# Attention scores in runs of nine over a ring of seven PSUM banks, with eight summed key blocks

## The chip, the core and the metric

The kernel runs on one core of a Trainium2 chip. The metric is the device time of one execution in microseconds, as the median of several runs. A core has a matrix engine (PE, TensorE; its weight loads are shown as PEld), a vector engine (DVE), a scalar engine (ACT), a general engine (POOL, GpSimd) and a sync engine (SP), and 16 DMA engines that the queues of SP and POOL share. Matrix products land in PSUM, which has eight banks of 512 fp32 numbers per partition; the rest lives in SBUF.

## The reference

Two layers are applied to an image tensor `x` of shape (2, 256, 64, 64). The change is in the first, which is plain attention over the 4096 pixels of each of the two images, with 8 heads of 32 channels:

```python
x = x + _L0_conv_ref(_gn(x), L0_conv_qkv_w, L0_conv_qkv_b, 8)

qkv = jnp.einsum('bchw,oc->bohw', x, qkv_w) + qkv_b[None, :, None, None]
qkv = qkv.reshape(b, 3, num_heads, head_dim, n)
q, k, v = (qkv[:, 0], qkv[:, 1], qkv[:, 2])
attn_logits = jnp.einsum('bhci,bhcj->bhij', q, k) * scale
attn_weights = jax.nn.softmax(attn_logits, axis=-1)
out = jnp.einsum('bhij,bhcj->bhci', attn_weights, v)
```

The second layer (group attention and a convolution over the result) is not changed.

## The kernel before

`attention0` handles one image. Its work is cut into 16 groups `g`: a head and one half of the 4096 queries, as four tiles of 512 queries. A group runs over 32 key blocks `j` of 128 keys. A **unit** is one key block against one query tile: a matmul of 128 keys by 512 queries, which fills one PSUM bank with scores. There are 16 x 32 x 4 = 2048 units for each image. A unit passes through these steps:

- PE writes the scores into a PSUM bank (`scores`, L505).
- ACT takes the exponential out of PSUM into SBUF (L511). The exponentials live in a ring of 28 places (`RING`), 17 of them in the tile `es` and 11 in the tile that also holds the values (shown as `v` in the profile). `at_places` splits an activation where the ring changes tile or wraps.
- PE multiplies them with the values and adds up in the bank `av` (`quarters`, L521), four query tiles side by side in four column groups of 32.
- For the softmax's denominator the exponentials of all key blocks have to be added. DVE adds most blocks into two tiles `e` (`add_rows`, L558). A few blocks of each group, listed in `SUMMED`, are added by POOL's accumulating DMAs into four tiles `acc` instead (`add_in_memory`, L566 for the first, which copies, and L568 for those that accumulate). At the start of the next group DVE adds `acc` to `e` (L748), and a matmul with ones sums over the partitions into a spare bank.

**Before**, `scores` issues seven units at a time into three PSUM tiles: `sa` of three banks, `sb` of two and `sc` of two, with one activation for each tile:

```python
for tag, size in (("sa", 3), ("sb", 2), ("sc", 2)):
    ...
    sc = psum["sc"].tile([P, size, T], F32, tag=tag, name=f"{tag}_{b}_{first}")
```

The eighth bank is `av`. When a spare bank is wanted (row sums of the group before, statistics of the next layer), `sa` is filled with two units and its third bank is lent.

The order on PE, ACT and DVE is written out by hand (`tc.manual_schedule`, from L771). Each turn of the loop issues one run of scores and then value products (`steps`, `work_of`) in half blocks: until the share that belongs to the scores issued so far is reached, and at least as many as `must` says, so that places of the ring that are about to be overwritten have been read. Value products work on units of earlier runs, never of the run just issued. DVE's additions stand in the order in which `work_of` asks for them. SP and POOL are ordered by the framework. SP fetches the next head's keys and values in every second group (`fetch_head`, asked for at `j == 4` of even groups) and the queries of the group after the next (`fetch_queries`).

A place of the ring is written again 28 places later. Before ACT may do so, PE's value product, DVE's addition and, in a summed block, the DMA that reads it must be done. An accumulating DMA waits for the one before it into the same tile of `acc`.

Of the kernel before, what the change touches and what calls it, by code (L numbers as in the profile page):

```python
# [9 lines left out]
F32 = mybir.dt.float32  # L10
I32 = mybir.dt.int32
F32R = mybir.dt.float32r
AF = mybir.ActivationFunctionType
# [4 lines left out]
P = 128  # L18
B, C, H, W = 2, 256, 64, 64
N = H * W  # L20
T = 512
# [4 lines left out]
NH0 = C // HD0  # L26
# [14 lines left out]
def direct_layers(ctx: ExitStack, tc: tile.TileContext, a: dict, out: bass.AP, bad: bass.AP):  # L41
# [3 lines left out]
    nc = tc.nc  # L45
# [11 lines left out]
    psum = {}  # L57
# [307 lines left out]
    SC0 = 1.0 / math.sqrt(HD0)  # L365
# [8 lines left out]
    NJ = N // P  # L374
# [76 lines left out]

    RING, RING_A = 28, 17

    SUMMED = (3, 7, 11, 15, 18, 22, 26)

    def summed(g):

        return SUMMED if g else SUMMED[1:]

# [4 lines left out]
    def attention0(b, xts, held):  # L464
# [10 lines left out]
        n_units = NH0 * 2 * NJ * 4  # L475
# [4 lines left out]
        places = []  # L480
        n_places = 0

        def at_places(first, n):

            while n > 0:
                at = first % RING
                m = min(n, (RING_A if at < RING_A else RING) - at)
                yield m, es[:, at : at + m, :] if at < RING_A else held["es"][:, at - RING_A : at - RING_A + m, :]
                first, n = first + m, n - m

        def scores(spare):

            nonlocal n_places
            bank = None
            for tag, size in (("sa", 3), ("sb", 2), ("sc", 2)):
                first = len(places)
                n = min(size - (spare and size == 3), n_units - first)
                if n <= 0:
                    break
                sc = psum["sc"].tile([P, size, T], F32, tag=tag, name=f"{tag}_{b}_{first}")  # L500
                if spare and size == 3:
                    bank = sc[:, size - 1, :]
                for i in range(n):
                    g, (j, u) = (first + i) // (4 * NJ), divmod((first + i) % (4 * NJ), 4)
                    nc.tensor.matmul(  # L505
                        sc[:, i, :], held["k", g // 2][:, j * P : (j + 1) * P], held["q", g, u // 2][:, u % 2, :],
                        start=True, stop=True,
                    )
                i = 0
                for m, dst in at_places(n_places, n):  # L510
                    nc.scalar.activation(dst, sc[:, i : i + m, :], AF.Exp, scale=SC0)  # L511
                    i += m
                places.extend(range(n_places, n_places + n))
                n_places += size
            return bank

        def quarters(dst, lhs, rhs, start, stop, part=None):

# [17 lines left out]
        def add_rows(g, j):  # L536
            if j == 0:
                sums[g] = psum["sc"].tile([P, T], F32, tag="av", name=f"av_{b}_{g}")
                added[g] = [w4([P, 2, T], f"e_{b}_{g}_{w}") for w in range(2)]
                return  # L540
            for w in range(2):
                dst = added[g][w]
                if j in summed(g):
                    if w == 0:
                        add_in_memory(g, j)
                    continue
                if j == 1:
                    first = two_units(g, 0, w), two_units(g, 1, w)
                    if len(first[0]) == len(first[1]) == 1:
                        nc.vector.tensor_add(dst, first[0][0][1], first[1][0][1])  # L550
                    else:
                        for s in range(2):
                            nc.vector.tensor_add(dst[:, s, :], unit(g, 0, 2 * w + s), unit(g, 1, 2 * w + s))
                    continue
                for s, src in two_units(g, j, w):
                    if g == last and j in SUMMED_LAST:
                        continue
                    nc.vector.tensor_add(dst[:, s, :], dst[:, s, :], src)  # L558
# [11 lines left out]
        def work_of(g, j):  # L570


            if (g, j) < (last, NJ - 3):
                add_rows(g, j)
            for part in (None,) if j in (0, NJ - 1) else range(2):
                if part == 1:
                    yield
                quarters(
                    sums[g], held["v"][:, (g // 2) % 2, j, :], lambda u: unit(g, j, u), j == 0, j == NJ - 1, part
                )  # L580

        def sum_rows(g, rows):
            if g == last:
                for part in range(2):
                    for j in SUMMED_LAST:
                        quarters(rows, ones, lambda u: unit(g, j, u), j == SUMMED_LAST[0], False, part)
                    quarters(rows, ones, lambda u: acc[u], False, False, part)
                    quarters(rows, ones, lambda u: added[g][u // 2][:, u % 2, :], False, True, part)
                return
            quarters(rows, ones, lambda u: added[g][u // 2][:, u % 2, :], True, True)  # L590
# [140 lines left out]
        def steps():  # L731

            for done in range(NH0 * 2 * NJ):
                g, j = divmod(done, NJ)
                if (g, j) == (last, NJ - 3):
                    assert len(places) == n_units
                    held["rows"] = psum["sc"].tile([P, 3, T], F32, tag="sa", name=f"rows_{b}")[:, 2, :]
                    for i in (NJ - 3, NJ - 2, NJ - 1):
                        add_rows(g, i)
                    sum_rows(g, held["rows"])  # L740
                for _ in work_of(g, j):
                    yield done
                if g and j == 0:

                    for w in range(2):
                        dst = added[g - 1][w]
                        for s in range(2) if w == 0 else (slice(0, 2),):
                            nc.vector.tensor_add(dst[:, s, :], dst[:, s, :], acc[s] if w == 0 else pair)  # L748
                    waiting.clear()
                if g and j == 1:  # L750
                    wanted.append(late[0].send)
                if g and j in (9, 17):
                    next(late[0])
                for what in also.get((g, j), ()):
                    what()
                if j == 4 and g % 2 == 0 and g // 2 + 1 < NH0:
                    fetch_head(b, g // 2 + 1, held)
                if j == NJ - 1:
                    waiting.append(g)
                    avs = w4([P, 2, T], f"avs_{b}_{g}")  # L760
                    if g < last:
                        nc.scalar.copy(avs[:, 0, :], sums[g])
                    copied[g] = avs
                    late[:] = [finish(g)]
                    next(late[0])
                    if g + 2 < NH0 * 2:
                        fetch_queries(b, g + 2, held)
                yield done + 1

        E = mybir.EngineType  # L770
        with tc.manual_schedule(engines={E.PE, E.Activation, E.DVE}):  # L771

            per_group = 2 * NJ - 2
            work, begun, taken = steps(), 0, 0
            scores(False)
            final = False
            while not final:
                have = len(places)  # L780
                use = wanted.pop(0) if wanted else None
                bank = scores(use is not None)
                final = have == n_units
                ready = have // 4
                share = have * per_group // (4 * NJ) - 2

                must = sum(place < n_places + 7 - RING for place in places[: 4 * ready : 4])
                if must % NJ == 1:
                    must += 1
                assert must <= ready  # L790
                here = 0
                while begun < ready and (taken < share or begun < must or final or use is not None):
                    if use is not None and here == 2:
                        use(bank)
                        use = None
                        continue
                    here += 1
                    group = begun // NJ
                    begun = next(work)
                    taken += 1  # L800
                    if begun // NJ > group and begun >= must and not final and use is None:
                        break
                if use is not None:
                    use(bank)
            assert next(work, None) is None
            return *finish_last(last), st
# [585 lines left out]
    for b in range(B):  # L1392
        xts = x_first if b == 0 else ahead["xts"]
        w0 = w0_first if b == 0 else ahead["w0"]
        with tc.tile_pool(name=f"ps0_{b}", bufs=8, space=PSUM) as psum["ps"]:
# [7 lines left out]
            held = project0(b, xn, w0)  # L1403
# [571 lines left out]
```

## Time and profile before

| | us |
|---|---|
| median of 3 runs | 3118.44 (3115.47 to 3122.96) |
| span of the profiled execution | 3116.4 |
| attention of the first image, first to last instruction | 118.4 to 1161.1 |
| attention of the second image | 1666.3 to 2709.4 |

| engine | busy us, whole span | share |
|---|---|---|
| PE | 3031.2 | 97% |
| DVE | 2467.0 | 79% |
| ACT | 2313.6 | 74% |
| POOL | 836.7 | 27% |

| group of instructions | count | mean ns |
|---|---|---|
| L505 scores, PE, `sa` / `sb` / `sc` | 1736 / 1180 / 1180 | 430 / 396 / 396 |
| L521 value products, PE, 256 queries | 15360 | 383 |
| L511 exponentials, ACT, two banks | 1180 in `sb` and `sc` | 1020 to 1037 |
| L511 exponentials, ACT, three banks | 556 | 1457 |
| L558 additions, DVE, 1024 wide | 1332 | 1216 |

A value product appears twice in the trace[...]. The durations of neighbouring instructions on one engine overlap, so that the distance from start to start, and not the duration, is what one of them costs in a full queue. DMA engines are busy for 80% of both attention stages.

### The profile page before, as it was taken

What the parts mean: (1) busy time and instruction counts of PE and PEld (TensorE: products, weight loads), DVE (VectorE), ACT (ScalarE), POOL (GpSimd) and SP (SyncE); (2) the same over time, 40 slices, a digit from 0 to 9 for tenths busy, and PEclk for the clock granted to TensorE, in tenths of its full rate; (3) what the DMA queues carried; (4) which work ended last, traced back from release to release, by engine and by line L of the source; (5) the groups of instructions that cost most, each with busy time, mean ns of one, the idle gap of its engine ahead of it and who ended that gap; (6) DMA issues with size and microseconds to landing.
All of it is one profiled execution on the core that took longest, in us unless ns stands there. A gap on an engine that the chain in (4) does not pass through costs nothing. (4 is left out here: it accounts for less than half of the span.)

```text
span 3116.4 us, 62659 instructions
## 1 busy us (share of the span) xinstructions
PE 3031.2 (97%) x25129; PEld 1830.6 (59%) x25129; DVE 2467.0 (79%) x3126; ACT 2313.6 (74%) x2436; POOL 836.7 (27%) x923
## 2 busy tenths in 40 slices
PE   6999999999999999999989999999999999999998
PEld 4555555555555556677755555555555555476765
DVE  4599989999899999856556998989989999834543
ACT  2699999999999984622237999999999999734333
POOL 2022222222222231055301222222222222305440
PEclk9999999999999999999999999999999999999999
DMA  7969679797897761230159687796888975700000
GB/s 241 270 132 185 143 150 172 154 178 150 164 181 154 145 133 33 75 134 29 41 193 268 128 176 151 156 176 138 177 162 164 181 153 123 170 4 4 21 14 22
DMA packets 243787, 424.41 MB, mean 136 GB/s; under 512 B 99112, under 2 KB 109916, under 8 KB 241308
## 3 DMA queue, kind: packets, MB, share of 16 engines
q0 software_dynamic: 94992, 238.36, 39.8%
q1 hardware_dynamic: 147580, 181.68, 21.6%
q8 instruction: 199, 3.26, 0.4%
q14 instruction: 104, 0.85, 0.1%
q10 hardware_dynamic: 912, 0.27, 0.0%
HBM read 119.03 MB, written 68.39 MB: 60 GB/s over the span
## 5 line engine op out<-in xcount | busy, mean ns | idle before, releaser
L558 DVE TENSOR_TENSOR e<-e,es 128x1024 f32<-128x1024 f32 (+1 forms) x956 | 1038.6, 1142 | 79.6 <-ACT es L511 77.9
L521 PE MATMUL av<-es,v 128*32 128x256 f32 (+1 forms) x9644 | 746.7, 390 | 0.0
L558 DVE TENSOR_TENSOR e<-e,v 128x1024 f32<-128x1024 f32 (+1 forms) x640 | 675.2, 1107 | 47.7 <-ACT v L511 46.6
L511 ACT ACTIVATE es<-sa 128x1536 f32<-128x1536 f32 (+1 forms) x444 | 635.7, 1432 | 93.1 <-PE sa L505 54.9
L505 PE MATMUL sa<-q,k 128*128 128x512 f32 x1736 | 561.4, 430 | 9.2 <-ACT avs L598 3.5
L521 PE MATMUL av<-v 128*32 128x256 f32 (+1 forms) x6228 | 506.5, 389 | 0.0
L521 PEld LDWEIGHTS av<-es,v 128*32 128x32 f32 x9644 | 316.1, 109 | 299.4 <-issue 160.6
L505 PEld LDWEIGHTS sa<-q,k 128*128 128x128 f32 x1736 | 280.0, 188 | 291.8 <-issue 135.4
L505 PE MATMUL sc<-q,k 128*128 128x512 f32 x1180 | 371.4, 396 | 1.7 <-ACT es L511 0.7
L505 PE MATMUL sb<-q,k 128*128 128x512 f32 x1180 | 371.0, 395 | 1.1 <-ACT es L511 1.1
L521 PEld LDWEIGHTS av<-v 128*32 128x32 f32 x6228 | 216.5, 109 | 178.6 <-issue 81.2
L511 ACT ACTIVATE es<-sc 128x1024 f32<-128x1024 f32 x296 | 306.9, 1037 | 0.0
L511 ACT ACTIVATE v<-sc 128x1024 f32<-128x1024 f32 x294 | 304.9, 1037 | 0.1
L511 ACT ACTIVATE es<-sb 128x1024 f32<-128x1024 f32 x296 | 302.0, 1020 | 3.8 <-DMA acc<-es 3.8
L511 ACT ACTIVATE v<-sb 128x1024 f32<-128x1024 f32 x294 | 300.0, 1020 | 0.0
L505 PEld LDWEIGHTS sb<-q,k 128*128 128x128 f32 x1180 | 221.2, 188 | 55.4 <-ACT es L511 2.9
L505 PEld LDWEIGHTS sc<-q,k 128*128 128x128 f32 x1180 | 210.5, 188 | 71.8 <-ACT es L511 12.1
L511 ACT ACTIVATE v<-sa 128x1536 f32<-128x1536 f32 (+1 forms) x146 | 209.2, 1433 | 35.6 <-PE sa L505 17.0
L948 PE MATMUL mm<-v,wf 128*128 128x256 f32 x1024 | 227.6, 380 | 1.5 <-DVE z L957 1.5
L568 POOL DMA_DIRECT2D es<-es x116 | 98.9, 853 | 475.6 <-ACT es L511 424.3
L948 PEld LDWEIGHTS mm<-v,wf 128*128 128x128 f32 x1024 | 193.3, 190 | 36.8 <-issue 9.9
L938 POOL TENSOR_TENSOR v<-col 128x512 f32<-128x512 f32 x128 | 165.1, 1316 | 179.2 <-ACT rk_sr L1089 39.2
(262 smaller groups left out, 3179.0 us busy)
## 6 DMA issues: line engine op xcount, KB each, us to landing
acc<-es POOLq DMA_DIRECT2D x128, 512.0 KB, 6.2
acc<-v POOLq DMA_DIRECT2D x84, 512.0 KB, 6.4
es<-es POOLq DMA_DIRECT2D x136, 256.0 KB, 4.5
v<-es POOLq DMA_DIRECT2D x132, 256.0 KB, 5.1
k<-wk_halves SPq DMA_DIRECT2D x64, 512.0 KB
q<-wq_halves SPq DMA_DIRECT2D x256, 128.0 KB
v<-v POOLq DMA_DIRECT2D x90, 256.0 KB, 5.4
es<-v POOLq DMA_DIRECT2D x86, 256.0 KB, 3.9
```

The lines of the kernel that those rows point to most:

```text
L505: nc.tensor.matmul(sc[:, i, :], held["k", g // 2][:, j * P : (j + 1) * P], held["q", g, u // 2][:, u % 2, :], start=True, stop=True,)
L511: nc.scalar.activation(dst, sc[:, i : i + m, :], AF.Exp, scale=SC0)
L521: nc.tensor.matmul(dst[HD0 * u : HD0 * u + HD0, n], lhs, rhs(u)[:, n], start=start, stop=stop)
L558: nc.vector.tensor_add(dst[:, s, :], dst[:, s, :], src)
L568: nc.gpsimd.dma_start(out=dst, in_=src, accum_op=ALU.add)
L938: (nc.gpsimd.tensor_add if plus else nc.gpsimd.tensor_sub)(dst, rows(one), rows(two))
L948: nc.tensor.matmul(mm[:, m, r, :], wf[:, k, 4 * r + q, m * P : (m + 1) * P], v[r // 2][:, r % 2, k, :], start=k == 0, stop=k == KC - 1,)
```

## The change

`sa`, `sb` and `sc` become one PSUM tile `ring` of seven banks, used in turn. A turn of the loop now issues nine units, in activations of 1, 1, 3, 2 and 2 banks (`PHASE`). Where such a part crosses the end of the ring of banks, or the end of a tile of exponentials, it is cut in two (`runs_of`). A spare bank is the next one of the ring and takes up one place. The loop keeps the value products at least seven units behind the scores (`behind`), and may carry on with them to the end of a group (`ending`). The list of summed blocks goes from seven of 32 key blocks to eight; in the first group of an image the first of the list is left out, as before.

```diff
-    SUMMED = (3, 7, 11, 15, 18, 22, 26)
+    SUMMED = (3, 6, 10, 13, 17, 20, 24, 27)
...
-        def scores(spare):
+        BANKS = 7
+
+        PHASE = (1, 1, 3, 2, 2)
+        ring = psum["sc"].tile([P, BANKS, T], F32, tag="ring", name=f"ring_{b}")
+
+        def spare_bank():
 
             nonlocal n_places
...
+            n_places += 1
+            return ring[:, (n_places - 1) % BANKS, :]
+
+        def runs_of(n):
+
+            at = n_places
+            while n > 0:
+                e = at % RING
+                m = min(n, BANKS - at % BANKS, (RING_A if e < RING_A else RING) - e)
+                yield at, m
+                at, n = at + m, n - m
+
+        def scores():
+
+            nonlocal n_places
+            for size in PHASE:
+                for at, m in list(runs_of(min(size, n_units - len(places)))):
+                    sc = ring[:, at % BANKS : at % BANKS + m, :]
+                    for i in range(m):
+                        unit = len(places) + i
+                        g, (j, u) = unit // (4 * NJ), divmod(unit % (4 * NJ), 4)
+                        nc.tensor.matmul(
+                            sc[:, i, :], held["k", g // 2][:, j * P : (j + 1) * P], held["q", g, u // 2][:, u % 2, :],
+                            start=True, stop=True,
+                        )
+                    ((_, dst),) = at_places(at, m)
+                    nc.scalar.activation(dst, sc, AF.Exp, scale=SC0)
+                    places.extend(range(at, at + m))
+                    n_places = at + m
...
-                    held["rows"] = psum["sc"].tile([P, 3, T], F32, tag="sa", name=f"rows_{b}")[:, 2, :]
+                    held["rows"] = spare_bank()
...
+            behind, reach = 7, sum(PHASE) + 1
             work, begun, taken = steps(), 0, 0
-            scores(False)
-            final = False
-            while not final:
-                have = len(places)
+            while begun < NH0 * 2 * NJ:
+                scores()
                 use = wanted.pop(0) if wanted else None
-                bank = scores(use is not None)
-                final = have == n_units
-                ready = have // 4
+                bank = spare_bank() if use is not None else None
+                final = len(places) == n_units
+                have = n_units if final else len(places) - behind
+                ready = max(0, have) // 4
                 share = have * per_group // (4 * NJ) - 2
 
-                must = sum(place < n_places + 7 - RING for place in places[: 4 * ready : 4])
+                must = sum(place < n_places + reach - RING for place in places[: 4 * ready : 4])
...
-                while begun < ready and (taken < share or begun < must or final or use is not None):
+                while begun < ready:
...
+                    ending = taken % per_group >= per_group - 2
+                    if not (taken < share or ending or begun < must or final or use is not None):
+                        break
+                    if not final and begun == NH0 * 2 * NJ - 3:
+                        break
```

The numbers of matmuls and of their rows are the same in both kernels. Lines move by some twelve: the exponentials are L525 in the changed kernel, the value products L533, DVE's additions L570, and the DMAs of the summed blocks L578 and L580.

More of the change, by code (lines that the diff above doesn't have):

```diff
@@ L489, in at_places @@
                 first, n = first + m, n - m
-        def scores(spare):
+        BANKS = 7
+        PHASE = (1, 1, 3, 2, 2)
+        ring = psum["sc"].tile([P, BANKS, T], F32, tag="ring", name=f"ring_{b}")
+        def spare_bank():
             nonlocal n_places
[L494 to L515, printed above, removed]
```

## The prediction

> **What bounds the kernel now.** I read the slices first, to see which stage carries the time.
>
> ```profile
> span 3116.4 us, 62659 instructions
> ...
> DVE  4599989999899999856556998989989999834543
> ACT  2699999999999984622237999999999999734333
> ...
> DMA  7969679797897761230159687796888975700000
> ```
>
> Two stretches, slices 2 to 15 and 22 to 35, have every engine near full: they are the attention of layer 0, once for each image. The change touches nothing else. Its first and last instructions bound it, and the windows view gives the load in it (busy time and number of instructions of PE, weight loads, DVE, ACT, POOL; then clock, DMA share, GB/s).
>
> ```profile
> 118.40:1161.10 1042.70, 1038.00 (x10188) 590.84 (x10188) 955.66 (x978) 972.15 (x921) 276.37 (x339) 1.00 0.80 161
> 1666.30:2709.40 1043.10, 1037.89 (x10188) 590.22 (x10188) 955.88 (x978) 971.96 (x921) 272.86 (x339) 1.00 0.80 160
> ```
>
> PE has 5 us of idle time in 1043, so 2085.8 us in both are PE's. A busy PE is not PE at its peak, so the third view is its timeline over one turn of the loop.
>
> ```profile
> 164.08 0.96 PE L505 MATMUL sa<-q,k 128*128 128x512 f32 x3
> 164.88 0.63 PE L505 MATMUL sb<-q,k 128*128 128x512 f32 x2
> 165.35 0.63 PE L505 MATMUL sc<-q,k 128*128 128x512 f32 x2
> 165.91 1.50 PE L521 MATMUL av<-v 128*32 128x256 f32 x24
> 167.23 0.61 PE L521 MATMUL av<-es,v 128*32 128x256 f32 x8
> 167.77 0.98 PE L505 MATMUL sa<-q,k 128*128 128x512 f32 x3
> ```
>
> Look at the starts. From sb to sc two scores take 0.47: 0.235 each. From sa to sb three take 0.80, so the first score after the value products costs 0.10 extra. From sc to av two take 0.56: 0.09 extra. From 165.91 to 167.23 six groups of four column tiles take 1.32; the steady group is 0.216, so 0.02 extra. The last two groups and the change back take 0.54: 0.11 extra. Over all turns of the trace the medians of these start-to-start distances are 337, 232, 327, 220, 196 and 309 ns, and the four extras sum to 0.335 us. **Each pair of switches between scores and value products costs PE 0.335 us.** The before order has 588 runs of scores: 197 us of the 2086 are switching.
>
> **What the Trainium skill says.** "TensorE: Matmul & The Clock Gate", Part 3, The mechanism: matmuls start and end strictly in order, so a score that waits for a bank holds all behind it. The trace agrees: where ACT is late, the score starts 53 ns after its activation's end, and what follows shifts with it. "ScalarE: Activation LUTs", What ACT_TABLE_LOAD costs: an ACTIVATE with immediate scale takes 186 ns + 0.833 ns an element, and neighbours overlap by about 93 ns; 512 columns would follow each other in some 520 ns. The trace is a little better:
>
> ```profile
> 189.16 0.61 ACT L762 COPY avs<-av 128x512 f32<-128x512 f32 x1
> 189.63 1.49 ACT L511 ACTIVATE es<-sa 128x1536 f32<-128x1536 f32 x1
> ```
>
> The next one starts 0.47 after a 512-wide copy (0.463 is the median of 30), 0.901 after a 1024-wide exponential and 1.348 after a 1536-wide one. So an activation costs 0.45 us a bank, however it is cut. "DMA: Bandwidth & Descriptors", Issuing engines are not separate DMA queues: transfers of SP and POOL share the same 16 engines. This trace agrees, and it matters below.
>
> **Part 1, runs of nine.** The two orders of instructions have 4096 scores and the same value products each. Runs of scores fall from 588 to 454 (450 of them of nine), so the change does what it says. 134 x 0.335 = **44.9 us less on PE**, all on the path.
>
> **Part 2, the spare bank.** In 12 places the first score of a turn waits for the copy of the row sums out of sa (L598), 0.36 us each, and in 4 for a copy of the statistics: 5.3 us. With the ring, the spare bank is written again only seven scores later: the **5.3 us** go. Another 4.2 us, 15 waits of an sc score for its exponential, I leave in.
>
> **Part 3, more and smaller activations.** Exponentials go from 1214 of two banks and 556 of three to 1392, 908 and 296 of one, two and three. By the distances above that is 1214 x 0.901 + 556 x 1.348 = 1843 us before, and 644 + 818 + 399 = 1862 after, plus 60 copies at 0.463 (28 us): 1890 of about 2036, or 93% against 90%. Does a run of nine fit seven banks? The eighth score falls on the bank of the first. Put the run's first score at 0: its exponential starts at 0.43 (the trace's distance) and ends at 1.02; the eighth score comes at 0.34 + 6 x 0.232 = 1.73. That leaves 0.7 us for a late ACT. A mean turn is 9 x 0.232 + 9 x 0.216 + 0.335 = 4.37 us, and ACT needs 9 x 0.45 = 4.07, so it catches up 0.3 a turn. I cost this at nothing; the 0.3 to 0.7 us cover it. Bounds: a gain of at most the 4.2 us left in part 2, if smaller activations free banks sooner; at the page's 0.52 ACT comes to 1969 us (97%) and some 10 us of PE waits follow; from 0.55 on ACT is the bound.
>
> **Part 4, the eighth summed block.** DVE loses 54 of 1332 wide additions (1.136 from start to start) and 20 narrow ones (0.602): 73 us. That is not on the path; DVE goes from 1911.5 busy to about 1838 of 2036, the same 90%. The price is on the DMA engines. One more block of 1 MB in each group (30 more in all), and a tighter chain: each accumulation into `acc` waits for the one before to land. Windows of half a group, first an even group (which fetches the next head's keys and values), then an odd one:
>
> ```profile
> 254.00:286.50 32.50, 32.50 (x330) 18.43 (x326) 29.93 (x33) 29.89 (x30) 9.78 (x13) 1.00 0.95 193
> 286.50:319.00 32.50, 32.50 (x313) 18.90 (x310) 30.26 (x31) 31.23 (x31) 7.98 (x10) 1.00 0.75 149
> 319.00:351.50 32.50, 32.23 (x316) 18.16 (x318) 29.62 (x30) 30.07 (x29) 10.33 (x13) 1.00 0.67 139
> 351.50:384.00 32.50, 32.50 (x322) 18.76 (x315) 30.30 (x29) 30.84 (x30) 6.83 (x9) 1.00 0.84 161
> ```
>
> In even groups the DMA engines are nearly full for the first half. The chain in one of them (issue of the pair's accumulation for blocks 11, 15, 18, 22, 26):
>
> ```profile
> 405.65 0.85 POOL L568 DMA_DIRECT2D acc<-es  x1 [1.78 <-ACT es L511]
> ...
> 413.40 0.86 POOL L568 DMA_DIRECT2D acc<-v  x1 [1.65 <-DMA acc<-es]
> ...
> 420.86 0.86 POOL L568 DMA_DIRECT2D acc<-es  x1 [3.06 <-ACT es L511]
> ...
> 426.33 0.86 POOL L568 DMA_DIRECT2D acc<-v  x1 [1.60 <-ACT v L511]
> ...
> 436.31 0.86 POOL L568 DMA_DIRECT2D acc<-es  x1 [3.66 <-ACT es L511]
> ```
>
> Over the 12 even groups 2 to 12 the four steps average 7.2, 6.3, 6.8 and 8.7 us, 29.0 in all; block 11 is issued 4.5 us after its exponentials, a transfer lands 6.7 later, and ACT writes the same places again 12.1 us after the exponentials. So 0.9 us is left, and the least is 0.1: ACT waits for `acc` six times, 5.6 us. After: blocks 10, 13, 17, 20, 24, 27, five steps. The extra one at the cheapest price makes 29.0 + 6.3 = 35.3 us; 17 blocks of (2086 - 50) / 1024 = 1.99 us give 33.8. The delay grows from 4.5 to 6.0; with 6.7 for landing it is 12.7 against 12.1: ACT waits 0.6 us. For the spread of the delays (2.3 to 5.4 us at block 26) I take 0.8, in 14 even groups (0 to 12 of both images): **11 us**, all passed to PE. Bounds: nothing, if block 6, now asked for 2 us earlier, lands ahead of the fetch; 3.6 us a group or more, if landings slow down. Odd groups delay their transfers 0.5 to 1.4 us only: no wait. Behind a waiting exponential stand all others on ACT, then PE's scores, since no bank comes free. POOL has nothing else queued there. `acc` is added to `e` at the next group's block 0 on DVE, where an accumulation that is late can cost DVE up to 2 us, inside its 10%.
>
> **Sum.** 3116.4 - 44.9 - 5.3 + 11 = 3077.2. The runs' median, 3118.4, stands 2.0 above the profiled span, so 3079.
>
> **Rivals.** *Transfers never late*: 3118.4 - 50.2 = 3068. For it: in odd groups the tightest block has 3.6 us left on average; against it: the 0.1 in even ones. *The accumulation chain becomes the bound of the even groups* (slower): with a mean step s and landing s - 0.6, the wait of a group is 4.5 + 5s - 33.8 + s - 0.6 - 12.1. At s = 7.6 it is 3.6 us, 14 of them eat the 50; at s = 8.0 it is 6.0, in all 84: 3118.4 - 50.2 + 84 = 3152. For it: the mean of the four steps is 7.25 already, and the even group's DMA load of (0.95 + 0.75) x 32.5 = 55 us of 65 rises by one block. That block's price is about 5.6 us (q0's 39.8% of 3116 us over 222 blocks), so 61 of 63.6. Against it: the last 8 blocks of a group have no accumulation, so there is room to drain. *ACT is slower on one bank than the copy shows* (0.55): 1392 x 0.087 = 121 us more, 2011 of 2036 busy, some 20 to 30 us of waits: 3105.
>
> **How the numbers follow.** A kernel like this can be told from no change beyond about 0.2%, 6 us. Chances: forecast 0.50, never late 0.20, chain bound 0.22, slow ACT 0.08. The forecast's own range is 3068 to 3100. The range 3060 to 3130 leaves out most of the chain case, about 0.17, and little below. Faster by over 0.2%: the first two and half of the last, less a tail of the forecast's waits: 0.70. Within: 0.07. Slower: 0.23.
>
> **What would show it.** Both attention stages shorten from 1043 to about 1023 us; score-to-score distances stay 232 ns and the extras 0.335; ACT's waits for `acc` grow from 5.6 to some 10 to 20 us, in even groups alone; waits for L598 are gone. I am wrong if one-bank exponentials follow each other in over 0.5 us, if PE's waits on ACT exceed 25 us, or if DVE's idle time before L570 doesn't stay near 127 us and ACT waits for DVE.

## The result: more than twice as slow

The changed kernel takes 6905.62 us (median, 6904.35 to 6910.22) against 3119.19 for the kernel before, a ratio of 2.2144 with a 95% interval of 2.2113 to 2.2176. The forecast was 3079 us. From the page of the changed kernel, the busy times and the slices:

```profile
span 6904.3 us, 63961 instructions
...
PE 4858.9 (70%) x25129; PEld 2229.2 (32%) x25129; DVE 2497.7 (36%) x3052; ACT 2597.8 (38%) x3262; POOL 938.4 (14%) x1043
...
PE   7666666666666666679986666666666666666799
...
ACT  3333333333333333334233333333333333333333
...
PEclk8666666666666666679986666666666666666799
DMA  7233332423242322222162323323232424222200
```

Before, every engine was near full in the two attention stages. Now none is: ACT, DVE and the DMA engines work a little over a third of the time at most, and PE two thirds, at a reduced clock. An engine that is too slow would be full; here the engines wait for each other. The windows over both stages (busy time of PE, weight loads, DVE, ACT, POOL; then clock, DMA share, GB/s) say that all of the loss is there:

```profile
119.00:3060.00 2941.00, 1954.66 (x10189) 790.49 (x10189) 973.36 (x942) 1116.37 (x1336) 329.54 (x399) 0.65 0.32 63
3560.00:6500.00 2940.00, 1953.50 (x10196) 790.60 (x10194) 974.97 (x945) 1117.69 (x1338) 324.95 (x399) 0.65 0.32 63
```

That is 5881 us instead of 2086; 1023 us lie outside, about as before. The timeline of one run of nine shows what waits for what (start, duration, engine, line, operation, tiles, count, and in brackets the idle time ahead of it with what ended it):

```profile
901.66 0.50 PE L520 MATMUL ring<-q,k 128*128 128x512 f32 x1
902.20 0.60 ACT L525 ACTIVATE v<-ring 128x512 f32<-128x512 f32 x1 [2.73 <-PE ring L520]
...
902.85 0.50 PE L520 MATMUL ring<-q,k 128*128 128x512 f32 x1 [0.69 <-ACT v L525]
903.39 0.60 ACT L525 ACTIVATE v<-ring 128x512 f32<-128x512 f32 x1 [0.59 <-PE ring L520]
...
904.04 1.06 PE L520 MATMUL ring<-q,k 128*128 128x512 f32 x3 [0.69 <-ACT v L525]
905.18 1.45 ACT L525 ACTIVATE v<-ring 128x1536 f32<-128x1536 f32 x1 [1.20 <-PE ring L520]
...
906.69 1.22 PE L520 MATMUL ring<-q,k 128*128 128x512 f32 x2 [1.59 <-ACT v L525]
...
907.94 1.02 ACT L525 ACTIVATE v<-ring 128x1024 f32<-128x1024 f32 x1 [1.31 <-PE ring L520]
```

The second score is for the next bank of the ring, and no one reads that bank. Still it starts at 902.85, some 50 ns after the exponential of the *first* bank has ended (902.20 + 0.60). The third part does the same with the second part, and so on. Over the whole trace the distance from the end of an exponential to the score after it is 52 to 53 ns in four of five parts; the others are the last parts of a run, where value products come between. PE and ACT take turns. A part of one bank takes 1.19 us here (0.54 from the score to its exponential, 0.60, 0.05) and 1.48 where the granted clock is lower (scores at 130.27, 131.75 and 133.23), where the forecast had 0.23 on PE beside 0.46 on ACT. The source view of the exponentials counts it, first the kernel after, then the one before:

```profile
its engine sat idle before it (us, times) until:
  PE ring L520: 3446.7, 2557
...
who waited for it (us, times):
...
  PEld ring L520: 2971.1, 2142
```

```profile
its engine sat idle before it (us, times) until:
  PE sa L505: 71.9, 120
...
who waited for it (us, times):
...
  PEld sa L505: 109.5, 225
```

ACT waits for a score ahead of 2557 of its 2596 exponentials; before it was 120 of 1770. The instruction stream agrees with the trace: in the changed kernel 2595 scores wait on ACT, 2560 of them for the newest exponential issued so far and 35 for other instructions of ACT. In the kernel before 1697 do, and for 1638 of them the exponential waited for is one or two older than the newest, because `sa`, `sb` and `sc` were three tiles.

So the suspicion after the result: the schedule orders PSUM accesses by *tile*, not by bank. With all seven banks in one tile, no score may be written while any bank of it still has to be read. "PSUM — Partial Sum Buffer", section "PSUM bank collisions raise a hardware error", asks for less than that: to guard PSUM by bank and quadrant. The traces agree that this is enough: in the kernel before, ACT reads `sa` from 165.08 to 166.54 while PE writes `sc` from 165.35 on.

### The profile page after: what moved, and what is told of

It is laid out like the page before. It is cut to its first block, busy times and chain, and to the rows that moved or that the text cites. A ratio compares the mean times of both kernels' runs of the same rounds, so it can differ in the third digit from the quotient of the medians.

```text
span 6904.3 us, 63961 instructions
## 1 busy us (share of the span) xinstructions
PE 4858.9 (70%) x25129; PEld 2229.2 (32%) x25129; DVE 2497.7 (36%) x3052; ACT 2597.8 (38%) x3262; POOL 938.4 (14%) x1043
## 5 line engine op out<-in xcount | busy, mean ns | idle before, releaser
L520 PE MATMUL ring<-q,k 128*128 128x512 f32 x4096 | 2224.3, 611 | 1970.7 <-ACT es L525 1200.9
L525 ACT ACTIVATE es<-ring 128x512 f32<-128x512 f32 (+2 forms) x1572 | 1334.1, 849 | 2099.6 <-PE ring L520 2095.5
L520 PEld LDWEIGHTS ring<-q,k 128*128 128x128 f32 x4096 | 898.9, 250 | 3294.1 <-ACT es L525 1809.1
L570 DVE TENSOR_TENSOR e<-e,es 128x1024 f32<-128x1024 f32 (+1 forms) x910 | 1042.0, 1154 | 2205.6 <-ACT es L525 2205.1
L525 ACT ACTIVATE v<-ring 128x512 f32<-128x512 f32 (+2 forms) x1024 | 855.2, 835 | 1356.7 <-PE ring L520 1351.2
L533 PE MATMUL av<-es,v 128*32 128x256 f32 (+1 forms) x9684 | 1240.6, 601 | 0.0
L570 DVE TENSOR_TENSOR e<-e,v 128x1024 f32<-128x1024 f32 (+1 forms) x612 | 676.2, 1116 | 1461.7 <-ACT v L525 1461.7
L533 PE MATMUL av<-v 128*32 128x256 f32 (+1 forms) x6188 | 852.6, 601 | 0.0
L533 PEld LDWEIGHTS av<-es,v 128*32 128x32 f32 x9684 | 466.7, 161 | 601.0 <-issue 580.8
L533 PEld LDWEIGHTS av<-v 128*32 128x32 f32 x6188 | 316.6, 162 | 378.2 <-issue 367.2
L580 POOL DMA_DIRECT2D es<-es x136 | 116.0, 853 | 1944.4 <-ACT es L525 1912.4
L580 POOL DMA_DIRECT2D es<-v x86 | 73.3, 853 | 1267.8 <-ACT v L525 1194.8
L965 PEld LDWEIGHTS mm<-v,wf 128*128 128x128 f32 x1024 | 193.3, 190 | 36.8 <-issue 9.8
L580 POOL DMA_DIRECT2D acc<-es x156 | 142.0, 910 | 215.2 <-ACT es L525 203.1
L580 POOL DMA_DIRECT2D v<-es x134 | 132.0, 985 | 118.2 <-ACT es L525 115.1
L578 POOL DMA_DIRECT2D es<-v x14 | 7.9, 567 | 783.3 <-ACT v L525 783.3
L578 POOL DMA_DIRECT2D es<-es x18 | 10.2, 569 | 727.8 <-ACT es L525 559.8
L580 POOL DMA_DIRECT2D acc<-v x96 | 86.5, 901 | 147.7 <-ACT v L525 146.1
L580 POOL DMA_DIRECT2D v<-v x88 | 83.0, 943 | 79.3 <-ACT v L525 77.9
```

Source lines behind the costliest of these rows:

```text
L520: nc.tensor.matmul(sc[:, i, :], held["k", g // 2][:, j * P : (j + 1) * P], held["q", g, u // 2][:, u % 2, :], start=True, stop=True,)
L525: nc.scalar.activation(dst, sc, AF.Exp, scale=SC0)
L533: nc.tensor.matmul(dst[HD0 * u : HD0 * u + HD0, n], lhs, rhs(u)[:, n], start=start, stop=stop)
L578: nc.gpsimd.dma_start(out=dst, in_=src)
L580: nc.gpsimd.dma_start(out=dst, in_=src, accum_op=ALU.add)
L965: nc.tensor.matmul(mm[:, m, r, :], wf[:, k, 4 * r + q, m * P : (m + 1) * P], v[r // 2][:, r % 2, k, :], start=k == 0, stop=k == KC - 1,)
```

## The experiments

### 1. One tile or several, with all else kept

First the changed kernel with seven tiles of one bank in place of one tile of seven, so that each part is one bank (`e1_seven_tiles`):

```diff
-        PHASE = (1, 1, 3, 2, 2)
-        ring = psum["sc"].tile([P, BANKS, T], F32, tag="ring", name=f"ring_{b}")
+        PHASE = (1,) * 9
+        ring = [psum["sc"].tile([P, 1, T], F32, tag=f"ring{i}", name=f"ring{i}_{b}") for i in range(BANKS)]
...
-                m = min(n, BANKS - at % BANKS, (RING_A if e < RING_A else RING) - e)
+                m = 1
...
-                    sc = ring[:, at % BANKS : at % BANKS + m, :]
+                    sc = ring[at % BANKS]
```

> The changed kernel with its ring of seven banks as seven PSUM tiles of one bank each, and every exponential of one bank (PHASE nine times 1). Theory (a score waits for the newest exponential of its whole PSUM tile, not of its own bank): the false waits are gone, runs of nine stay, so 3060 to 3110 us, attention about 1015 to 1035 us an image, granted clock about 0.99. Rival A (seven banks are too few for runs of nine, so that scores really wait for their own bank's reader): stays above 5000 us. Rival B (the eighth summed block's accumulating DMAs hold ACT up): stays near 6900 us, since they are unchanged.

Then the reverse, in the kernel before: `sa`, `sb` and `sc` as slices of one tile of seven banks (`e3_before_one_tile`), and as a control three tiles that are allocated once and kept, so that only the number of tiles differs between the two (`e3c_before_kept_tiles`):

```diff
+        BANKS3 = {"sa": (0, 3), "sb": (3, 2), "sc": (5, 2)}
+        seven = psum["sc"].tile([P, 7, T], F32, tag="seven", name=f"seven_{b}")
+        parts3 = {t: seven[:, lo : lo + n, :] for t, (lo, n) in BANKS3.items()}
...
-                sc = psum["sc"].tile([P, size, T], F32, tag=tag, name=f"{tag}_{b}_{first}")
+                sc = parts3[tag]
```

> The kernel before (runs of seven, activations of 3, 2 and 2 banks, seven summed blocks), where sa, sb and sc are slices of one PSUM tile of seven banks. No bank changes its reader or its order. Theory of the whole-tile wait: each of the three parts of a turn waits for the exponential of the part before; a turn takes 9 to 10 us in place of 3.5, and the kernel 6000 to 6800 us, with a granted clock of 0.65 to 0.75. Rival A (banks too few) and rival B (DMAs): no change, 3110 to 3130 us.

> The control of the one before: sa, sb and sc are three PSUM tiles as in the kernel before, but allocated once an image, not once a turn, as the slices of the one tile are. All theories: 3110 to 3130 us. If it is much slower, keeping a tile is what costs, not sharing it.

Measured: seven tiles 3119.26 us, ratio to the kernel before 1.0006 (0.9997 to 1.0015). The kernel before with one tile 5831.76, its control 3121.56 (one run each). The groups of the scores in the one-tile run, and one of the control's (count, busy time and mean ns, idle time ahead of them and what ended it):

```profile
L509 PE MATMUL seven<-q,k 128*128 128x512 f32 x4096 | 1745.9, 525 | 1584.1 <-ACT es L515 1022.3 <-ACT v L515 556.5 <-ACT avs L602 3.2
```

```profile
L508 PE MATMUL sa<-q,k 128*128 128x512 f32 x1736 | 561.3, 430 | 9.2 <-ACT avs L601 3.5 <-ACT es L514 2.9 <-DVE hl_wq L413 1.6
```

What follows: the cause is shown from both sides. One tile alone makes the kernel before slow, with its runs of seven, its activations and its DMAs untouched; taking the one tile away cures the changed kernel. The price per part is about the same: (5831.8 - 3118) / 1770 parts = 1.53 us there, (6905.6 - 3118) / 2596 = 1.46 us in the changed kernel. So the cut into five or six parts a run, 2596 in place of 1770, made the loss larger. The one-tile run came out a little below the 6000 to 6800 us expected, and far from the 3110 to 3130 of both rivals.

But the 50 us that the forecast put on the runs of nine didn't come back: the cured kernel takes as long as the one before, and misses the 3060 to 3110 us expected of it.

### 2. The eighth summed block

The cured kernel with the seven summed blocks of before (`e2_seven_tiles_old_sum`), and the changed kernel with them (`e4_after_old_sum`):

```diff
-    SUMMED = (3, 6, 10, 13, 17, 20, 24, 27)
+    SUMMED = (3, 7, 11, 15, 18, 22, 26)
```

> As the kernel with seven one-bank tiles, but with the list of seven summed blocks of before. It tells the price of the eighth block where the runs of nine work. The prediction's step: ACT's waits for acc (some 11 us) go, and DVE has 73 us more to do in a stage of 2036 us: 5 to 15 us faster than with eight blocks. Rival: DVE, at 94% of the stage, becomes the bound or holds places of the ring longer: 10 to 40 us slower than with eight blocks.

> The changed kernel with the seven summed blocks of before. Theory (the wait on the whole seven-bank tile is the whole loss): as the changed kernel, 6880 to 6930 us, attention stages of 2940 us. Rival (the eighth summed block's DMAs carry a part of the loss): clearly shorter, below 6800 us.

Measured: 3119.6 us (ratio 1.0005, 0.9998 to 1.0011), and 6908.86 (one run). In both settings the eighth block has no net effect. It neither caused the loss nor ate the gain of the cured kernel, and both expectations for the cured kernel (5 to 15 us faster, or 10 to 40 slower) were missed. What ACT waits for says more, first in the cured kernel with eight blocks, then with seven:

```profile
its engine sat idle before it (us, times) until:
  PE ring L520: 12.2, 29
  DMA acc<-v: 4.7, 7
  DMA acc<-es: 4.1, 7
```

```profile
its engine sat idle before it (us, times) until:
  PE ring L520: 13.9, 30
  DVE e L570: 6.1, 2
  DMA acc<-es: 1.4, 2
```

With seven blocks ACT waits 7.4 us less for `acc`, but 6.1 us for DVE's additions come up. The two about balance, though the second figure rests on two waits of one execution.

### 3. Where the gain of the runs of nine went

In the cured kernel (`e1_seven_tiles`) the windows over both stages, from the first score to the last, and one row of ACT's timeline:

```profile
119.20:1154.80 1035.60, 1031.40 (x10048) 603.35 (x10051) 911.32 (x933) 1021.95 (x2078) 328.29 (x398) 1.00 0.89 178
1670.70:2705.90 1035.20, 1033.23 (x10048) 603.35 (x10052) 911.49 (x933) 1021.26 (x2078) 324.64 (x398) 1.00 0.89 177
```

```profile
612.90 8.56 ACT L525 ACTIVATE es<-ring 128x512 f32<-128x512 f32 x17
```

The fourth busy time is ACT's: 1022 of 1035 us, where the kernel before has 968 of the same length:

```profile
118.00:1153.00 1035.00, 1029.92 (x10040) 586.13 (x10044) 948.83 (x969) 968.39 (x918) 276.23 (x338) 1.00 0.80 162
```

PE is full too, so it takes the start-to-start distances to see who leads. ACT's row shows 17 exponentials without a gap. Their starts are 477 ns apart, their ends 490 (over 3600 such pairs in the trace), so each is recorded as 13 ns longer than the last: 0.72 us for the first of these and 0.92 for the last. A bank comes free at the end. 2048 exponentials at 0.490 are 1003 us of a stage of 1035, and with 30 copies of some 0.48 it is 1018. This makes ACT the likely bound.

Four runs test this. Runs of eight (`e5_runs_of_eight`): `PHASE = (1,) * 8`. Tiles of 1, 1, 2, 2, 1 banks with runs that end at a tile's edge (`e6_wider_tiles`), whose core is

```diff
+        WIDTHS, LIMIT = (1, 1, 2, 2, 1), 9
+        TILE = [t for t, w in enumerate(WIDTHS) for _ in range(w)]
+        ring = [psum["sc"].tile([P, w, T], F32, tag=f"ring{i}", name=f"ring{i}_{b}") for i, w in enumerate(WIDTHS)]
...
+            left = LIMIT
+            while len(places) < n_units and WIDTHS[TILE[n_places % BANKS]] <= left:
```

and exponentials of 384 columns, to take load off ACT alone (`e7_narrow_exps`), then with runs of seven (`e11_narrow_sevens`, `PHASE = (1,) * 7`):

```diff
-                    nc.scalar.activation(dst, sc, AF.Exp, scale=SC0)
+                    wide = T if at < RING else 3 * T // 4
+                    nc.scalar.activation(dst[:, :, :wide], sc[:, :, :wide], AF.Exp, scale=SC0)
```

> Seven one-bank tiles, runs of eight in place of nine. Theory X (ScalarE is the bound with one-bank parts: in the run with runs of nine its exponentials end 489 ns apart when they stand back to back, 2048 of them are 1002 us of a stage of 1035 us, and PE then waits for banks, some 20 us before scores and 12 us before weighted sums): a run of eight asks for its eighth bank later against ScalarE's progress and leaves ScalarE more time per score, so the stage takes 1023 to 1029 us and the kernel 3096 to 3108 us, although PE switches 28 times more per image. Rival Y (longer runs save nothing, because a switch is dearer or cheaper than read or each awaited bank costs PE by itself): 3117 us or more.

> Tiles of 1, 1, 2, 2, 1 banks and runs of up to nine that end at a tile's edge (eight or nine), so that about half of the scores are evicted two at a time. Theory X: ScalarE's own need falls from 1002 to some 970 us per image, PE's stalls are then those on a two-bank tile that a run uses twice, about 16 us; stage 1025 to 1031 us, kernel 3100 to 3112 us. Rival Y (longer runs save nothing): 3117 us or more.

> Seven one-bank tiles, runs of nine, and after the first 28 units of an image each exponential covers 384 of the 512 columns; the other columns of es keep older values. PE, DVE and DMA do all their work as in the run with full exponentials. Theory X (ScalarE is what holds the runs of nine back): exponentials end some 0.38 to 0.40 us apart, PE hardly waits for banks, the stage falls from 1035 to 1010 to 1016 us and the kernel to 3070 to 3082 us, which is the gain that was forecast for the runs of nine. Rival Y: no change, 3112 us or more. Rival Z (the DMA engines, 0.89 busy, or DVE bound the stage): no change either, 3112 us or more.

> The run with exponentials of 384 columns, with runs of seven in place of nine: 66 more switches each way per image, ScalarE far from its bound. If a pair of switches costs the 0.335 us that the prediction used: 3070 + 2 x 66 x 0.335 = 3114 us (3108 to 3118). If longer runs save nothing by themselves: 3068 to 3076 us.

Measured: runs of eight 3110.7 us (ratio 0.9983, 0.9973 to 0.9992), wider tiles 3151.18 (1.0117, 1.0102 to 1.0133), narrow exponentials 3070.36 (0.9848, 0.9833 to 0.9863), narrow with runs of seven 3104.61 (0.9953, 0.9938 to 0.9968).

Runs of eight gained a little, but missed the 3096 to 3108 expected.

With a quarter of the exponentials' columns left out, and all of PE's, DVE's and DMA's work kept, the gain of the runs of nine is there: 48 us with the eighth block, where the forecast had 39. ACT has become the bound of the cured kernel. This run gives ACT more room than the forecast assumed (exponentials end 0.383 us apart, and not 0.45), so it shows that ACT held the gain back, not what a kernel with whole exponentials can reach. The source view of this run's exponentials says that ACT now waits for PE, as it did in the kernel before:

```profile
its engine sat idle before it (us, times) until:
  PE ring L520: 292.4, 391
  DMA acc<-es: 21.6, 18
  DMA acc<-v: 13.1, 13
```

That DMA or DVE bound the cured kernel is ruled out: here they do the same work in less time. That longer runs save nothing is ruled out by the runs of seven, 34 us slower than those of nine. This is less than the 44 us of the full price, below the 3108 to 3118 expected; the table below shows the rest as less waiting. The wider tiles were expected at 3100 to 3112 and are slower than before; this expectation was wrong. ACT has room there (busy for some 996 of 1046 us), but PE stops at some 145 scores inside the runs of an image (101 with seven tiles and runs of nine, 17 before). After 119 of these stops the next score, which needs no further wait, comes about 337 ns later instead of 232. So such a stop costs 0.1 us beyond its wait: 12 us an image, which the estimate had left out. The stops themselves take 29 us, and not the 16 expected; why, no run shows.

To see it in one table, I compare each start-to-start distance on PE with its usual value (232 ns between scores, 337 after the first of a run, 309 from value products to a score, 327 back) and add up what is above it by more than 20 ns. This excess is time that PE waits or loses after a wait. Per image, mean of two:

| kernel | runs of scores | first score to last, us | PE's excess, us | difference of the two |
|---|---|---|---|---|
| before | 294 | 1034.7 | 12.9 | 1021.8 |
| seven tiles, nine | 227 | 1035.4 | 36.8 | 998.6 |
| seven tiles, eight | 255 | 1029.2 | 20.9 | 1008.3 |
| wider tiles | 233 | 1046.4 | 45.9 | 1000.5 |
| narrow, nine | 227 | 1010.8 | 14.4 | 996.4 |
| narrow, seven | 292 | 1027.6 | 8.8 | 1018.8 |

The last column follows the number of runs: from 294 to 227 it falls by 23.2 us, or 0.35 for a pair of switches; between the narrow runs by 22.4 for 65 runs, 0.34. The prediction's 0.335 stands. (A switch that became dearer would count as excess, so the column alone shows only that none became cheaper.) The times of the narrow runs agree: 34 us, and 11 for the excess that the runs of seven save in both images, are 0.35 us for each of 130 pairs. In the cured kernel the 23 us saved per image are the 24 us of excess added.

### 4. What the eighth block costs when ACT has room

The narrow run again, with the old list of summed blocks (`e10_narrow_old_sum`, same diff as in 2):

> The run with exponentials of 384 columns (ScalarE far from its bound), with the seven summed blocks of before in place of eight. If the eighth summed block costs what the prediction put on it (11 us of ScalarE's waits for accumulating DMAs in each image): 3050 to 3060 us. If that cost is hidden while ScalarE has room: 3066 to 3074 us, as with eight. If DVE's 60 adds more are on the path: 3080 us or more.

Measured: 3062.64 us (3059.62 to 3066.75), 7.7 less than with eight blocks (3068.78 to 3071.18), between two of the bands expected. The same source view:

```profile
its engine sat idle before it (us, times) until:
  PE ring L520: 303.7, 403
  DMA acc<-v: 4.7, 4
...
  DMA acc<-es: 1.3, 4
```

With eight blocks ACT waits 34.7 us for the accumulating DMAs (21.6 + 13.1, 31 times), with seven 6.0. PE's excess is 14.4 us an image with eight and 8.4 with seven. So the eighth block has a price as soon as ACT isn't the bound. How large it is stays less sure: the two runs' ratios to the kernel before, 0.9848 (0.9833 to 0.9863) and 0.9824 (0.9809 to 0.9840), overlap, and PE's excess says 12 us in both images. In the cured kernel the price isn't seen (experiment 2): ACT's waits for `acc` are 8.8 us with eight blocks, and with seven those for DVE take their place.

### 5. A version ahead of both

Runs of eight gained a little, so I moved the value products of that kernel: they follow 6 (`e8_eight_behind_6`) or 4 (`e9_eight_behind_4`) units behind the scores instead of 7. Against the kernel with seven tiles:

```diff
-        PHASE = (1,) * 9
+        PHASE = (1,) * 8
...
-            behind, reach = 7, sum(PHASE) + 1
+            behind, reach = 6, sum(PHASE) + 1
```

> As the run with one-bank tiles and runs of eight, with the weighted sums following 6 units behind the scores in place of 7, so that their half blocks fall at other places between the runs. Theory (ScalarE and the eighth bank set the pace, and how often PE stops for a bank depends on how evenly the sums lie between the runs; each stop costs its wait and 0.1 us more): fewer stops, stage 1022 to 1026 us, kernel 3096 to 3106 us. Rival (ScalarE's own need of some 1020 us is the floor and the place of the sums has no effect): 3107 to 3114 us, as with 7.

> The same with 4 units in place of 7. Theory: 3096 to 3106 us. Rival: 3107 to 3114 us. A third way: with 4 units the first sums of a run may find their exponentials not done, PE then waits before sums, 3115 us or more.

Measured: 3097.26 us with 6 (ratio 0.9928, 0.9914 to 0.9942) and 3102.96 with 4 (0.9947, 0.9933 to 0.9960). Both stages with 6:

```profile
118.10:1143.10 1025.00, 1022.93 (x10040) 600.57 (x10042) 908.55 (x924) 1018.58 (x2077) 327.46 (x397) 1.00 0.90 179
1658.00:2681.10 1023.10, 1022.53 (x10040) 599.35 (x10044) 908.21 (x924) 1017.94 (x2077) 323.63 (x397) 1.00 0.89 179
```

The theory held: PE's excess falls from 20.9 us an image (7 units) to 16.4 and 17.1. With 6 units ACT is busy for 1018 of 1024 us, so little is left in this design; what it gains is 0.7%. The same with seven summed blocks wasn't tried.

## Why the prediction was wrong

**The step that failed is in Part 3**: "The eighth score falls on the bank of the first ... That leaves 0.7 us for a late ACT." It took for granted that a score waits for the last reader of its own bank. That was never read: neither in the instruction stream, where each score's wait names the exponential it is for, nor by asking what the three tiles of before did besides holding banks. They were what let PE write `sb` while ACT read `sa`. The trace of before showed scores that started 53 ns after "their" exponential, and I read this as a wait by bank; it is the same with a wait by tile, as long as a tile is one activation. The runs showed a wait by tile in its place: every part of a run waits for the exponential of the part before, about 1.46 us for each of 2596 parts. The step "I cost this at nothing" was worth 3800 us.

**The rivals.** None was this case. The slower ones were an accumulation chain, which has no part in the loss (6908.86 with seven blocks), and a slower ACT, which is no part of it either: in the changed kernel it idles for most of both stages. The remark that it could be wrong "if PE's waits on ACT exceed 25 us" names the sign (PE waited 1967 us for ACT), but gave it no mechanism and no chance.

**Part 1** held in its price (0.34 to 0.35 us for a pair of switches against 0.335) and in its count; the saving arrives once ACT has room.

**Part 2** held as far as it can be seen: in the cured kernel, first scores of a run that come late fall from 24 to 15 per image and from 6.1 to 3.2 us, 5.8 us in both images against the 5.3 forecast.

**Part 3's price of one bank** was too low as well. 0.463 us came from copies, from start to start. Exponentials start 0.477 apart and end 0.490 apart, so that "0.45 us a bank, however it is cut" doesn't hold. "ScalarE: Activation LUTs", What ACT_TABLE_LOAD costs, gave an estimate of 0.52; the trace lies between. With all parts of one bank, 27 ns on 4096 exponentials are 111 us, and they made ACT the bound of the cured kernel. Whether the changed kernel's own cut of 1, 1, 3, 2 and 2 banks would reach the forecast with waits by bank wasn't tried: its activations reach over any two or three neighbouring banks, and fixed tiles of several banks, as in the wider tiles, don't give that.

**Part 4** held in part. ACT's waits for `acc` do grow with the eighth block. That it costs 7.7 us where ACT has room, against 11, is in part luck: ACT waits 34.7 us for `acc` there and not 10 to 20, 3.8 of them in odd groups, and most of the added waiting doesn't reach the time. That DVE's saving is worth nothing isn't shown: with seven blocks ACT waits 6.1 us for DVE in the cured kernel, with eight not at all. Two small slips move nothing: 9 x 0.45 is 4.05 and not 4.07, and DVE's 1911.5 of 2086 us are 92%.

## What to carry to other kernels

Before you merge buffers, find out by what unit the schedule keeps them apart: read for each writer which reader its wait names, before and after. Where the newest reader is named each time, two engines will take turns, whatever the banks are. And when a wait is taken away, price the next engine in its new cut: one-bank parts were safe for the waits and made ACT the bound.

## What the runs showed of the hardware

- One-bank exponentials without a gap start 477 ns apart but end 490 apart, so a series of them shows durations from 0.59 to 1.02 us. What waits for the end sees 490: in the cured kernel, when two scores in a row are stopped, the second comes about 490 ns after the first (49 pairs).
- A score that follows a stopped one comes after about 337 ns and not 232, if its own bank is free (the wider tiles, 119 times in an image). The extra 0.1 us is as long as what the first score after value products costs.
- A PE that waits often is slow while it works. "TensorE: Matmul & The Clock Gate", Part 1, What's actually happening, says that the clock runs at half rate when PE hasn't been busy enough. The trace agrees: the granted clock is 0.65 in the changed kernel's stages, made of stretches at full and at half rate, and a group of four value products mostly starts 427 ns after the one before it, where the kernel before has 216.
